# Two neighbouring keys per partition in a two-layer cross-attention kernel on one Trainium2 core

## The chip, the cores and the metric

The kernel runs on one core of one Trainium2 chip. The metric is the device time of one execution in microseconds (us); lower is better. The engines are named as the profile names them: PE is TensorE's matmul, PEld its weight load, DVE is VectorE, ACT ScalarE, POOL GpSimd, and SP is SyncE, whose queue issues nearly all loads from HBM. A stretch of the trace is given as the two times, in us from the start of the span, between which it lies.

## The reference

Two cross-attention layers are applied one after the other to `x` (8 batches, 100 tokens, 1024 features). Both attend to the same context `ctx_512` (8 batches, 1444 keys, 512 features). Everything is float32.

```
# layer 0
Q = x @ Wq + bq ; K = ctx @ Wk + bk ; V = ctx @ Wv + bv
w = softmax(Q @ K.T / 32, over the 1444 keys)
x = x + (w @ V) @ Wo + bo
# layer 1, with its own weights
q, k, v = as above
w = softmax(q @ k.T / 32, over the 100 tokens)
x = layer_norm(x + w @ v) * gamma + beta
```

The context appears in two roles. In the scores the sum runs over features, and each key is an output. In the weighted sum of the context the sum runs over keys. A sum over keys does not depend on the order in which the keys are taken, as long as the weights and the context rows use the same order.

## The kernel before, in words

**Algebra.** Keys and values are never formed. The product `Wq Wk^T` is made once per layer and applied to `x`, which gives for each token a query of 512 features, `gT[layer]`. Scores are then products of these queries with the raw context, and the weighted sums of the raw context (512 features per token, the tile `A`) are multiplied by `Wv` (layer 1) or `Wv Wo` (layer 0) behind the attention. The dense products use sub-products with fewer multiplications than the plain form.

**Order.** The span falls into these stages: weight products, queries and preparations of both layers (0 to 181 us), attention of layer 0 (181 to 306), output of layer 0 and queries of layer 1 (306 to 383), attention of layer 1 with its output in between (383 to 547), the last tokens (547 to 571). TensorE's instructions are in the order of the program (`manual_schedule` for PE). Loads of the context go through `loaded_in_order` (L947 to L955), which keeps them in program order on the SP queue and makes each wait, so that no more than `UNDER_WAY` (1800 KB), itself included, is on its way at any time:

```
while sum(size for _, size in under_way) > UNDER_WAY:
    latest, _ = under_way.pop(0)
```

**Two copies of the context.** For the scores the features must be on the partitions. The host gives the context also transposed, and `load_features` (L957) brings it as four tiles `cT` per batch, one per 128 features, each with all 1444 keys in its columns (two loads per tile in layer 0, four in layer 1). For the weighted sums the keys must be on the partitions. `load_rows` (L977) brings the context as it is, as four tiles `c` ("units") per batch. A unit holds three key tiles of 128 keys, side by side in the columns, 512 features each. So `c` has on partition p, key tile i of unit q, the key `384 q + 128 i + p`. The last unit holds two full key tiles and the last 36 keys. There are twelve key tiles m, numbered through: unit `m // 3`, place `m % 3`.

**Scores** (`scores_by_keys`, L1076 to L1109). For each of the four feature chunks k and each key tile m, the weights of the matmul are 64 columns of `cT[k]`, and the 100 queries of the batch are what moves through the array. A full key tile is made in two halves of 64 keys, one on each half of the array's columns, so that the two matmuls overlap in time. Scores of key tile m go to column block m of three PSUM banks, with the key's place in the tile as partition. A float32 matmul shows as two records in the trace, each with its own weight load. Softmax follows on DVE and ACT, and leaves the weights `w[p, m, token]`.

**Weighted sums** (`weighted_rows`, L1009 to L1059). For each key tile and feature chunk, 64 columns of `c` are the weights of the matmul and `w[:, m, :]` moves. Again there are two halves.

**Together** (`alternated`, L1533). Weighted sums of batch b and scores of batch b + 2 take turns on TensorE, a step of each at a time: 48 steps per batch, of four records of `A` (L1020) and four of `s` (L1092). The loads of batch b's rows and of batch b + 2's features take turns on the SP queue in the same way: the rows of one unit, then one feature tile (`loaded`, L1525).

Of the kernel before, what the change touches and what calls it, by code (L numbers as in the profile page):

```python
# [31 lines left out]
P = 128  # L32
HP = P // 2
# [5 lines left out]
CQ = MC // NQ  # L39
# [19 lines left out]
def two_layer_cross_attention(ctx: ExitStack, tc: tile.TileContext, a: dict, out: bass.AP):  # L59
# [11 lines left out]
    def bank(name):  # L71
        return psum.tile([P, 512], F32, tag="ps", name=name)
# [4 lines left out]
    def unit(name):  # L77
        return stream.tile([P, E + L], F32, tag="unit", name=name)

    def wide(name):  # L80
        return work.tile([P, LC, GT], F32, tag="AT", name=name, bufs=2)
# [4 lines left out]
    def weight_rows(name):  # L86
        return work.tile([P, MC * T], F32, tag="wT", name=name, bufs=3)
# [859 lines left out]
    def loaded_in_order(to, src):  # L947

        load = tc.keep_in_program_order(nc.sync.dma_start(out=to, in_=src)).ins
        under_way.append((load, 4 * math.prod(to.shape)))  # L950
        latest = None
        while sum(size for _, size in under_way) > UNDER_WAY:
            latest, _ = under_way.pop(0)
        if latest is not None:
            tc.add_manual_dep(load, latest.name, landed, reason="room among the transfers under way")  # L955

    def load_features(b, blocks=(2, 3), parts=2, order=range(LC)):  # L957

        bounds = [LAST * i // parts for i in range(parts)] + [S]

        for k in order:
            name = f"cT_{b}_{k}"
            t = feature_block(name) if k in blocks else unit(name)[:, :S]
            for part in (slice(i, j) for i, j in zip(bounds, bounds[1:])):
                loaded_in_order(t[:, part], a["ctxT"][b][k * P : (k + 1) * P, part])
            yield t

    def quarters_of(b):

        return (NQ - 1, *range(NQ - 1)) if b in SECOND else range(NQ)  # L970

    def last_rows(b):

        p0 = HP if b in SECOND else 0
        return slice(p0, p0 + S - LAST)

    def load_rows(b):  # L977

        src = a["ctx_512"][b]
        for q in quarters_of(b):  # L980
            t = unit(f"c_{b}_{q}").rearrange("p (c l) -> p c l", c=CQ)
            n = CQ - (q == NQ - 1)
            r0 = q * CQ * P
            for i in range(n):
                loaded_in_order(t[:, i, :], src[r0 + i * P : r0 + (i + 1) * P, :])
            if n < CQ:
                more = PAD - (S - LAST)
                loaded_in_order(t[last_rows(b), n, :], src[LAST:S, :])
                if b not in FIRST + SECOND:
                    loaded_in_order(t[S - LAST : PAD, n, :], src[:more, :])  # L990
            yield t

    def keys(m):

        return P if m < MC - 1 else S - LAST
# [3 lines left out]
    def both_sides():  # L999

        return side, 1 - side

    def one_side():

        nonlocal side
        side = 1 - side
        return (1 - side,)
# [68 lines left out]
    def scores_by_keys(s, layer, cT, softmax, hold=False):  # L1076

        b = s["b"]
        q = gT[layer][b // G]
        t0 = b % G * T  # L1080
        banks = [bank(f"s{layer}_{b}_{n}") for n in range(MC // GM)]
        rest = []
        for k in range(LC):
            for m in KEYS:
                whole = keys(m) == P
                n = HP if whole else keys(m)
                for h in both_sides() if whole else one_side():
                    o = m * P + h * HP if whole else m * P
                    to = banks[m // GM][h * HP : h * HP + n, m % GM * T : (m % GM + 1) * T]
                    if k >= LC - 2 and not whole:  # L1090
                        rest.append(to)
                    nc.tensor.matmul(  # L1092
                        to,
                        cT[k][:, o : o + n],
                        q[:, k, t0 : t0 + T],
                        start=(k == 0 and m % GM == 0),
                        stop=(k == LC - 1 or (k == LC - 2 and not whole)),
                        skip_group_check=True,
                    )
                if hold or (k, m) != (LC - 1, KEYS[-1]):  # L1100
                    yield
        w = weight_rows(f"w{layer}_{b}")
        s["w"] = w[:, : MC * T].rearrange("p (c t) -> p c t", t=T)
        if b not in FIRST + SECOND:
            nc.gpsimd.memset(s["w"][:PAD, MC - 1, :], 0.0)
        s["softmax"] = softmax(s, [blocks_of(banks, ms) for ms in ROWS], rest)
        for _ in islice(s["softmax"], LATER.get((layer, b))):
            pass
        yield  # L1109

    def blocks_of(banks, ms):

        m, n, r = ms[0], len(ms), keys(ms[0])
        ps = banks[m // GM][:r, m % GM * T : (m % GM + n) * T]
        return ms, slice(0, r), ps.rearrange("p (c t) -> p c t", t=T)
# [417 lines left out]
    def alternated(b, layer, softmax, dst, first=0, got=None):  # L1533

        nxt = b + 2 < B
        rows = batches[b].pop("rows", None) or load_rows(b)
        c, *cT = got or loaded(rows, *([load_features(b + 2, parts=4 if layer else 2)] if nxt else []))
        if b in FIRST:
            other, more = batches[b + 1], load_rows(b + 1)
            other["first"] = next(more)  # L1540
            other["rows"] = chain([other["first"]], more)
        A = weighted_rows(batches[b], layer, c, dst)
        ahead = scores_by_keys(batches[b + 2], layer, *cT, softmax) if nxt else iter(())
        run(islice(ahead, first))
        for n in range(MC * LC):
            if n < (LC * (MC - 1) if b in FIRST else LC * MC):
                next(A, None)
            next(ahead, None)
            if n == LC * MC - 1:
                next(A, None)  # L1550
            yield

    cT = [list(load_features(0))]
    block, *more = load_features(1, (2,), order=(2, 0, 1, 3))
    cT.append([*more[:2], block, *more[2:]])
    c0, more = list(load_rows(0)), load_features(2)
    cT.append([next(more)])
    scores0 = scores_by_keys(batches[0], 0, cT[0], softmax0)
    run(islice(scores0, 3 * MC + 6))
    run(key_bias_rows(kb0, part0, bqbk0))  # L1560
    run(scores0)
    cT[2] += more
    block_sums("u1", acc_u, sums[:, :LC, :], late=True)
    block_sums("wqbk1", acc_c, sums[:, LC : LC + EC, :], late=True)
    run(scores_by_keys(batches[1], 0, cT[1], softmax0))
    for b in range(B):
        dst = A0[b // G][:, :, b % G * T : (b % G + 1) * T]
# [44 lines left out]
    cT = [list(load_features(0, parts=4)), list(load_features(1, (2,), 4))]  # L1612
    result = out.rearrange("b t e -> (b t) e")
    n = TILES[-1][0] // 6
# [32 lines left out]
    for b in range(B):  # L1647
        parts = []
        for last, _, tokens in SETS:
# [3 lines left out]
            if last not in homes:  # L1653
                t = wide(f"A1T_{last}").rearrange("p c t -> p (c t)")[:, : LC * len(tokens)]
# [52 lines left out]
```

## Time and profile before

| | us |
|---|---|
| median of 3 runs | 571.9 |
| lowest and highest | 570.89 and 572.43 |
| the profiled execution's own time | 573.0 |
| its span, first to last instruction | 571.2 |

Stages of the profiled execution, as busy times in us:

| stretch | PE | PEld | DVE | DMA share | GB/s |
|---|---|---|---|---|---|
| 0 to 181 | 179.85 | 143.29 | 152.49 | 0.86 | 234 |
| 306 to 383 | 77.00 | 53.50 | 60.63 | 0.60 | 198 |
| 547 to 571.2 | 16.51 | 13.13 | 14.51 | 0.28 | 56 |

The two stages of attention are shown with the prediction. Loads of the context in the profile, by size and with the median time from issue to landing:

| load | count | KB each | us to landing |
|---|---|---|---|
| rows, one key tile of 128 keys | 176 | 256 | 4.8 |
| rows, the last 36 keys | 16 | 72 | |
| features, layer 0, columns 0 to 703 | 32 | 352 | 4.7 |
| features, layer 0, columns 704 to 1443 | 32 | 370 | 4.6 |
| features, layer 1, three parts of 352 columns | 96 | 176 | 4.7 |
| features, layer 1, the last 388 columns | 32 | 194 | 4.8 |

How to read it: the mean of a group in the profile is the time of one instruction from its start to its end, not what it adds to the stream. Matmuls and weight loads overlap in time, so a group's mean is longer than its step; the step is read from the starts in the timeline. The busy time is the union of such intervals. A waiting time is put down to the instruction or landing that ended it; "issue" means that the profile shows nothing that it waited for. The DMA share is the mean busy share of the core's 16 DMA engines.

### The profile page before, as it was taken

How to read it: one execution, taken by the hardware profiler on the slowest of the kernel's cores; microseconds unless marked ns; L12 is line 12 of the kernel's file. 1: busy time of each engine (PE TensorE's matmuls, PEld its weight loads, DVE VectorE, ACT ScalarE, POOL GpSimd, SP SyncE). 2: the span in 40 equal slices, each digit the busy share in tenths (PEclk: the TensorE clock that was granted, in tenths of full speed). 3: DMA queues.
4: the chain of work that ended last, by engine and by line, in shares of the span. 5: the costliest groups of instructions: out<-in, count | busy, mean ns of one | idle time of the engine just before them, and what ended most of it. 6: DMA issues, size and time to landing. Idle time of an engine off the chain costs nothing.

```text
span 571.2 us, 17345 instructions
## 1 busy us (share of the span) xinstructions
PE 560.2 (98%) x7328; PEld 471.2 (82%) x7328; DVE 453.2 (79%) x1051; ACT 146.0 (26%) x383; POOL 112.9 (20%) x171
## 2 busy tenths in 40 slices
PE   9999999999999999999999999999999999999994
PEld 8887567668999989999997856679999869959672
DVE  2997979878999794886457687799788779879865
ACT  1331321356020112202111000121433035336632
POOL 3110110222100043142222000000421312403232
PEclk9999999999999999999999999999999999999998
DMA  9959989958938999899999503985899969985804
GB/s 287 318 109 322 309 208 279 318 90 199 254 66 296 331 330 332 293 325 328 326 329 318 196 1 129 288 298 189 253 293 336 341 208 325 312 271 169 220 5 92
DMA packets 73390, 141.24 MB, mean 247 GB/s; under 512 B 8160, under 2 KB 29920, under 8 KB 73312
## 3 DMA queue, kind: packets, MB, share of 16 engines
q1 hardware_dynamic: 66592, 121.40, 62.6%
q0 software_dynamic: 6288, 18.20, 16.5%
q8 instruction: 58, 0.95, 0.7%
q10 hardware_dynamic: 432, 0.52, 0.3%
q14 instruction: 20, 0.16, 0.1%
HBM read 123.49 MB, written 6.03 MB: 227 GB/s over the span
## 4 chain that ended last, share of the span: by engine, by line
PE 77%; DMA 18%; issue 2%; DVE 1%; SPq 1%; POOL 1%; ACT 1%; DVEq 0%; POOLq 0%
DMA cT<-in_ctxT 14%; PE A L1020 14%; PE s L1092 12%; PE qk_x L170 7%; PE g_x L170 6%; PE vo_x L170 4%; DMA c<-in_ctx 4%; PE o_x L170 3%; PE o_x L1343 3%; PE qk_z L170 2%; PE g_y L170 2%; PE o_y L1343 2%; PE o_y L170 1%; PE qk_w L170 1%; PE qk_y L170 1%
## 5 line engine op out<-in xcount | busy, mean ns | idle before, releaser
L1020 PE MATMUL A<-w,c 128*64 128x100 f32 (+2 forms) x3072 | 217.0, 249 | 1.7 <-issue 1.7
L1020 PEld LDWEIGHTS A<-w,c 128*64 128x64 f32 (+2 forms) x3072 | 190.1, 137 | 4.8 <-issue 3.6
L1092 PE MATMUL s<-g1T,cT 128*64 128x100 f32 (+1 forms) x1472 | 109.5, 249 | 0.0
L1092 PE MATMUL s<-g0T,cT 128*64 128x100 f32 (+1 forms) x1472 | 108.3, 249 | 0.5 <-DMA cT<-in_ctxT 0.5
L1092 PEld LDWEIGHTS s<-g1T,cT 128*64 128x64 f32 (+1 forms) x1472 | 94.9, 136 | 0.8 <-DMA cT<-in_ctxT 0.6
L1092 PEld LDWEIGHTS s<-g0T,cT 128*64 128x64 f32 (+1 forms) x1472 | 94.2, 136 | 1.0 <-DMA cT<-in_ctxT 0.7
L1310 POOL TENSOR_TENSOR part<-w 128x500 f32<-128x500 f32 x16 | 25.3, 1584 | 237.0 <-DVE rtotal L102 77.9
L1288 ACT ACTIVATE w<-w,negmax 128x100 f32<-128x100 f32 x96 | 34.9, 365 | 44.5 <-DVE negmax L102 44.2
L1156 ACT ACTIVATE w<-w 128x400 f32<-128x400 f32 (+2 forms) x32 | 12.8, 447 | 115.5 <-DVE w L102 104.7
L102 DVE STREAM_TRANSPOSE z<-xT 32x256 f32<-32x256 f32 x88 | 38.3, 435 | 1.4
L170 PE MATMUL qk_x<-qk 128*128 128x256 f32 x160 | 37.8, 380 | 0.0
L170 PEld LDWEIGHTS qk_x<-qk 128*128 128x128 f32 x160 | 28.9, 190 | 3.4 <-ACT qk L444 0.2
L1073 DVE RECIPROCAL rrow<-A 128x100 f32<-128x100 f32 x8 | 6.2, 770 | 22.7 <-PE A L1064 22.6
L170 PE MATMUL vo_x<-vo 128*128 128x512 f32 x48 | 23.3, 594 | 0.0
L102 DVE TENSOR_REDUCE most<-s 128x100 f32<-128x400 f32 (+1 forms) x24 | 12.6, 525 | 10.9 <-PE s L1092 10.3
L102 DVE TENSOR_TENSOR w<-w,rtotal 128x400 f32<-128x400 f32 (+2 forms) x32 | 18.2, 567 | 1.1
L102 DVE SCALAR_TENSOR_TENSOR w<-s,kb 128x400 f32<-128x400 f32 (+2 forms) x32 | 14.3, 464 | 5.4 <-PE s L1092 5.1
L742 ACT ACTIVATE g1T<-g_x,k 128x400 f32<-128x400 f32 x4 | 2.4, 593 | 61.0 <-PE g_x L170 60.9
L1288 ACT ACTIVATION_READ_ACCUMULATOR w<-w,negmax 128x1 f32 x96 | 17.9, 187 | 0.0
L1313 POOL TENSOR_TENSOR part<-part 128x100 f32<-128x100 f32 x32 | 15.8, 493 | 2.5
L102 DVE TENSOR_TENSOR qk<-qk 128x256 f32<-128x256 f32 (+2 forms) x27 | 14.9, 579 | 0.0
L170 PE MATMUL qk_z<-qk 128*128 128x256 f32 x64 | 14.1, 379 | 0.0
(490 smaller groups left out, 1010.2 us busy)
## 6 DMA issues: line engine op xcount, KB each, us to landing
c<-in_ctx SPq DMA_DIRECT2D x176, 256.0 KB, 4.8
cT<-in_ctxT SPq DMA_DIRECT2D x96, 176.0 KB, 4.7
cT<-in_ctxT SPq DMA_DIRECT2D x32, 370.0 KB, 4.6
cT<-in_ctxT SPq DMA_DIRECT2D x32, 352.0 KB, 4.7
cT<-in_ctxT SPq DMA_DIRECT2D x32, 194.0 KB, 4.8
vo<-in_L_xattn_Wo SPq DMA_DIRECT2D x8, 512.0 KB, 9.0
qk<-in_L_xattn_WqT SPq DMA_DIRECT2D x8, 512.0 KB, 6.3
qk<-in_L_xattn_WqT SPq DMA_DIRECT2D x15, 256.0 KB, 4.9
```

The costliest lines, as they stand in the source:

```text
L102: ins = getattr(nc.vector, op)(*args, **kw)
L170: nc.tensor.matmul(banks[n // per][:, n % per * width : (n % per + 1) * width], lhs[i][:, n * P : (n + 1) * P], rhs[i], start=(fresh and i ...
L742: nc.scalar.activation(dst[g][:, c, :], banks[j][:, :GT], AF.Identity, bias=u[:, c : c + 1])
L1020: nc.tensor.matmul(ps[h * HP : (h + 1) * HP, k * T : (k + 1) * T], block[rows, m % CQ, k * P + h * HP : k * P + (h + 1) * HP], s["w"][rows ...
L1073: nc.vector.reciprocal(r, ps[:, GT : GT + T])
L1092: nc.tensor.matmul(to, cT[k][:, o : o + n], q[:, k, t0 : t0 + T], start=(k == 0 and m % GM == 0), stop=(k == LC - 1 or (k == LC - 2 and no ...
L1156: nc.scalar.activation(rows, rows, AF.Exp)
L1288: ins = nc.scalar.activation(rows[:, i, :], rows[:, i, :], AF.Exp, bias=negmax[:, i : i + 1], accum_out=total[:, i : i + 1])
L1310: add(part, w[:, 0:5, :], w[:, 5:10, :], ALU.add)
L1313: add(part[:, 0, :], part[:, 0, :], more, ALU.add)
L1343: nc.tensor.matmul(ps[:n, :], lhs[0][:, i, :], rhs[0][:, i, :], start=(fresh and i == 0), stop=(i == 1), skip_group_check=True,)
```

## The change

In `load_rows` the first two key tiles of each unit are loaded with one transfer of 256 keys, viewed so that partition p takes the two neighbouring keys `384 q + 2 p` and `384 q + 2 p + 1`. The first goes to place 0, the second to place 1; the two keys are 4096 contiguous bytes in HBM and in the partition. The third key tile, where there is one, and the last 36 keys are loaded as before. The number of bytes is the same.

In `scores_by_keys` the order of the scores follows. For places 0 and 1 of a unit (m = 0, 1, 3, 4, 6, 7, 9 and 10) the weights are taken from a block of 256 columns of `cT[k]`, every second column, beginning at column 0 or 1 of the block; the 128 columns of a key tile are again cut in two halves of 64. For place 2 (m = 2, 5, 8) and for the last 36 keys the columns are contiguous as before. Number, shape and order of all matmuls are the same, and so are softmax and weighted sums in the program's text.

```
@@ load_rows
-            for i in range(n):
-                loaded_in_order(t[:, i, :], src[r0 + i * P : r0 + (i + 1) * P, :])
+            pair = src[r0 : r0 + 2 * P, :].rearrange("(p c) l -> p c l", c=2)
+            loaded_in_order(t[:, :2, :], pair)
+            if n > 2:
+                loaded_in_order(t[:, 2, :], src[r0 + 2 * P : r0 + n * P, :])
@@ scores_by_keys
-                    o = m * P + h * HP if whole else m * P
+                    block = cT[k][:, m * P : m * P + keys(m)]
+                    if whole:
+                        if m % CQ < 2:
+                            o = m // CQ * CQ * P
+                            block = cT[k][:, o : o + 2 * P].rearrange("p (i c) -> p c i", c=2)[:, m % CQ, :]
+                        block = block[:, h * HP : (h + 1) * HP]
...
                     nc.tensor.matmul(
                         to,
-                        cT[k][:, o : o + n],
+                        block,
                         q[:, k, t0 : t0 + T],
```

## The prediction

> **What bounds the kernel now.** I read the page first, then the busy time by stage, then the waits of TensorE and of the SP queue, then TensorE's timeline at its longest data wait, and last the matmul and weight-load groups by shape.
>
> ```profile
> PE 560.2 (98%) x7328; PEld 471.2 (82%) x7328; DVE 453.2 (79%) x1051; ACT 146.0 (26%) x383; POOL 112.9 (20%) x171
> PE 77%; DMA 18%; issue 2%; DVE 1%; SPq 1%; POOL 1%; ACT 1%; DVEq 0%; POOLq 0%
> ```
>
> TensorE is busy for 98% of the span, so 11.0 us at most are idle in it. Yet 18% of the chain that ended last is DMA: two resources are nearly balanced. The stages say where (columns: us, then busy us and count of each engine, granted clock, DMA share, GB/s):
>
> ```profile
> 181.00:306.00 125.00, 122.80 (x2855) 121.09 (x2853) 89.01 (x234) 19.58 (x40) 31.56 (x52) 1.00 0.96 323
> 383.00:547.00 164.00, 164.00 (x2949) 140.16 (x2948) 136.59 (x308) 59.99 (x237) 42.03 (x66) 1.00 0.80 256
> ```
>
> The first row is the attention of layer 0, the second that of layer 1; the granted clock is full in both. In layer 0 the DMA engines are busy for 96% and TensorE lacks 2.2 us; in layer 1 TensorE lacks nothing. All that TensorE waits for behind the start is this:
>
> ```profile
> PE A L1020 <- issue: 1.7, 2, 1.2
> PE s L1092 <- DMA cT<-in_ctxT: 0.5, 1, 0.5
> SPq L949 <- DMA cT<-in_ctxT: 40.9, 43, 3.1
> SPq L949 <- DMA c<-in_ctx: 18.0, 33, 2.4
> ```
>
> The two last lines are the SP queue in 181 to 306: it waits 58.9 us for room among the transfers under way, not for buffers. The one data wait stands at the end of 107 us of full DMA:
>
> ```profile
> 287.77 0.34 PE L1020 MATMUL A<-w,c 128*64 128x100 f32 x4
> 287.95 0.34 PE L1092 MATMUL s<-g0T,cT 128*64 128x100 f32 x4
> 288.12 0.34 PE L1020 MATMUL A<-w,c 128*64 128x100 f32 x4
> 288.99 0.39 PE L1092 MATMUL s<-g0T,cT 128*64 128x100 f32 x4 [0.53 <-DMA cT<-in_ctxT]
> ```
>
> Groups of four records start every 0.171 us: 42.8 ns a record, 85.6 ns for a pair, one on each column half (matmuls of 64 columns on the two halves overlap). The group at 288.99 was due at 288.29: 0.7 us lost. One batch of layer 0 loads 2888 KB of rows and 2888 KB of features, 5.91 MB, 18.3 us at 323 GB/s; TensorE needs 48 steps of 0.342 us, 16.4 us. So the lead won before 181 us melts by about 1.9 us a batch and is gone at 288 us. That matters twice: a faster DMA can win back 0.7 us and no more, a slower one is paid nearly in full.
>
> **The change: the weight loads.** Each matmul here has two records and two weight loads (92 matmuls a batch, 1472 records in 8 batches). In 8 of 11 full key tiles the weights come from every second column: 8 x 2 sides x 4 chunks x 2 records x 16 = 2048 records, 1024 pairs. Count, shape and order stay. What a load costs:
>
> ```profile
> L1092 PEld LDWEIGHTS s<-g0T,cT 128*64 128x64 f32 x1408 | 90.4, 137 | 1.0 <-DMA cT<-in_ctxT 0.7
> L1092 PEld LDWEIGHTS s<-g0T,cT 128*36 128x36 f32 x64 | 6.4, 113 | 0.0
> L170 PEld LDWEIGHTS qk_q_x<-qk 128*128 128x128 f32 x48 | 6.0, 192 | 0.1
> ```
>
> The mean goes 113, 137, 192 ns for 36, 64, 128 columns: 0.86 ns per column on both steps, so 64 columns take 55 ns and the rest is latency. It has to fit under one record of the same half, 85.6 ns. A strided load may therefore take 85.6/55 = 1.56 times as long and cost nothing; what hides it is the matmul running on that half, and behind 1.56 each extra ns is paid by every pair. No load of before is strided, so I bound it. Below: nothing; a gain is excluded, as the column count is the same and loads already end in time. Above: twice the time, 110 ns; the nearest row is a load of 128 columns under 128 moving ones, whose eight records start 0.89 us apart, 111 ns each. 111 - 85.6 = 25.4 ns, x 1024 = 26 us. The Trainium skill, "SBUF — State Buffer", section on the DMA port swizzle, has the rule that speaks against the change: SBUF is read in lines of 16 bytes, an access that crosses to a new line pays, and full rate needs two or more accesses per line. Unit stride gives four float32 per line, every second column two: crossings double, the condition is just met. By its limit the term is 0, by its penalty up to 26 us. No run here shows which. I take 0, since rule and 1.56 would both have to fail, and keep 26 us as the far end.
>
> **The transfers.** Per batch and layer the row loads go from 11 of 256 KB (and the small ends) to 4 of 512 KB and 3 of 256 KB; bytes are the same. The SP queue saves 64 issues in all at a median of 402 ns (the rows' tile view), 26 us of its time; worth nothing, since it waits for landings anyway. Each row packet becomes 4096 bytes instead of two of 2048. In the trace's packet records of 182 to 289 us a 2048-byte packet takes 94.1 ns on average, 84 ns in the median; 4096-byte packets of the same queue, elsewhere in this trace, 159 ns in the median. Ratio 159/168: two rows go from 188 to 178 ns. 8238 row packets fall in that stretch, 8/11 paired: about 3000 pairs x 10 ns / 16 engines = 1.9 us. The Trainium skill, "DMA: Bandwidth & Descriptors", "Why small descriptors are slow", gives about 3 cycles a packet beside one per 32 bytes: 131 instead of 134, 2.2%, estimate 0.8 us. Measurement first, 1.9; but the sum is the same by either, for both cover the 0.7 us wait and there is nothing further to win. Where that wait goes, TensorE itself is next.
>
> **The added granularity.** The first tile of a unit now waits for 512 KB: it can start 256 KB / 323 GB/s = 0.8 us later, if rows are what comes last. They aren't: no wait for c is in TensorE's list, and each unit's rows are issued ahead of the feature tile needed at the same step, which decides. With room for 1800 KB, a steady cycle of 352, 370, 256, 256, 256 KB leaves at least 1120 KB in flight while SP waits; with the pair it is 978 KB when the next pair is to go. Behind a waiting pair stand its third tile and the next feature loads. 978 KB is 3.1 us of work, against 2.5 us from issue to landing of the fastest load: still covered, cost 0; with the cover gone see below.
>
> Other edits are nil: buffers, softmax and the final row ends keep their order; a sum over keys doesn't mind their permutation. The two "issue" stops (2.1 us between starts, at 202 and 301, each inside a group of four, so no data) I leave.
>
> **Sum.** Weight loads 0, data wait -0.7, granularity 0. Profiled: span 571.2 to 570.5, run 573.0 to 572.3. That run lies 1.1 above the median of 571.9, so I predict 571.2 us.
>
> **The rivals.** *Strided weight loads are slower than the matmul that covers them.* For: PEld is busy for 121 of 125 us in layer 0, the cover is 31 ns wide, and line crossings double. Against: two accesses per line and room for 1.56 times. From 1.56 on it decides; at twice, 26 us: 597 us; at 1.75 times, 96 ns, 11 us: 582.
>
> *The coarser queue starves the DMA engines.* For: SP spends 76 waits on landings in 125 us, the cycle is DMA-bound, and 978 KB leave just 0.6 us of margin. A bubble of 0.2 us in each of some 20 cycles is 4 us, all paid: about 575. Against: 64 fewer issues, longer packets.
>
> *More than the wait is won.* If emptier queues also end the two "issue" stops, 2.1 us more go: 569.1. For: both lie where DMA is full. Against: nothing ties them to context data.
>
> *The change does nothing to the packets* (the pair is still cut into rows): 571.9, no change.
>
> **How the numbers follow.** 0.3%, 1.7 us, is about what a measurement of this kernel can tell from no change. Covered loads with the won wait: 0.40, of which 0.35 same and 0.05 faster by spread. Packets unchanged: 0.05, same. More won, some part of the stops: 0.21, all faster. Starved DMA: 0.12, 0.10 slower and 0.02 same. Slow weight loads: 0.22, all slower, a third of it below 580. Sums: faster 0.26, same 0.42, slower 0.32. The range starts at 569.2, leaving out 0.04, and ends at 580, leaving out about 0.15 of slow loads; the covered cases alone are 569.2 to 573.
>
> **What would show it.** Right: strided loads may read longer than 137 ns, but groups in layer 0 still start 0.171 us apart; row packets of 4096 bytes, about 8200 fewer packets; the wait at 288 us is gone; DMA share a little under 0.96. Wrong by the first rival: groups of scores start more than 0.171 us apart in key tiles 0, 1, 3, 4, 6, 7, 9, 10 and not in 2, 5, 8, and both attention stages grow alike. By the second: pace kept, but new waits of TensorE for c or cT in layer 0 alone, with the DMA share below 0.95.

## The result, and the profile after

The changed kernel takes 576.02 us (median of 11 runs, 572.53 to 578.85), the kernel before 571.89 us in the same session (median of 11). The ratio is 1.0061, with a 95% interval from 1.0037 to 1.0085: slower by 3.5 us, between 2.1 and 4.9 (the two medians lie 4.1 us apart). Forecast were 571.2 us and no change; the range (569.2 to 580) holds the result, the direction is not the one forecast. The profiled execution took 575.32 us with a span of 573.5 us, close to the median. Two of the six runs by halves of the partitions were more than 1.5% slower than the fastest of them and are left out of its numbers.

The page of the changed kernel, busy times and the chain that ended last:

```profile
PE 561.1 (98%) x7328; PEld 471.8 (82%) x7328; DVE 452.7 (79%) x1051; ACT 145.9 (25%) x383; POOL 113.1 (20%) x171
PE 88%; DMA 7%; issue 1%; DVE 1%; POOL 1%; ACT 1%; SPq 0%; DVEq 0%; POOLq 0%
```

TensorE's busy time is 0.9 us higher and the span 2.3 us longer, so most of the loss is idle time. The share of DMA in the chain fell from 18% to 7%, although DMA is what got worse. In both traces the chain leaves TensorE at its last wait for data and follows the loads back from there; before, it stays with them from 289 to 182 us, after, only from 292 to 250 us, where a load had waited 0.3 us for a buffer that TensorE freed, and it returns to TensorE. This share does not measure what DMA costs. The busy time by stage does better (us, then busy us and count of PE, PEld, DVE, ACT, POOL, granted clock, DMA share, GB/s):

```profile
181.00:306.00 125.00, 121.07 (x2799) 119.14 (x2799) 85.79 (x223) 18.09 (x36) 31.10 (x51) 1.00 0.91 310
383.00:547.00 164.00, 164.00 (x2950) 140.94 (x2950) 138.47 (x310) 59.84 (x236) 39.91 (x61) 1.00 0.82 263
```

In the attention of layer 0 the DMA engines are busy for 91% of the time instead of 96% and move 310 GB/s instead of 323. Over 125 us that is 1.6 MB less, 5 us of transfers. TensorE lacks 3.9 us there, all for data, instead of 2.2, of which 0.5 were for data. In layer 1 it lacks nothing, before or after. TensorE's waits for data, of its list of waits (us in total, times, longest):

```profile
PE s L1099 <- DMA cT<-in_ctxT: 3.9, 5, 1.2
```

And what the SP queue waits for in 181 to 306, in the same columns:

```profile
SPq L949 <- DMA c<-in_ctx: 48.4, 29, 3.3
SPq L949 <- DMA cT<-in_ctxT: 23.6, 30, 1.8
```

There was one data wait of 0.5 us; now there are five, 3.9 us. SP's waits for landed rows went from 18.0 us to 48.4 us, with fewer of them: a wait for a pair is long. In sum SP waits for 72.0 us instead of 58.9, while the DMA engines move less. The last of the five waits in TensorE's timeline:

```profile
290.55 0.25 PE L1022 MATMUL A<-w,c 128*64 128x100 f32 x1
290.63 0.25 PE L1099 MATMUL s<-g0T,cT 128*64 128x100 f32 x1
290.64 0.41 PE L1022 MATMUL A<-w,c 128*64 128x100 f32 x3
292.29 0.39 PE L1099 MATMUL s<-g0T,cT 128*64 128x100 f32 x4 [1.24 <-DMA cT<-in_ctxT]
292.51 0.34 PE L1022 MATMUL A<-w,c 128*64 128x100 f32 x4
```

It stands at a score, not at a weighted sum: the rows, whose loads were changed, arrive in time, and the feature tile queued behind them comes late.

The trace's packet records show where the DMA engines ran dry. In the mean over 18 pairs between 195 and 282 us their busy share falls to 0.78, 0.71 and 0.66 in the second, third and fourth quarter of a microsecond after SP issues the pair; in the kernel before it is 0.91 or more in the first 1.25 us after the first row load of a unit. In the records one can also count what is issued and not yet moved. When SP issues a pair, that is 463 KB in the mean (19 pairs between 195 and 286 us), though the program counts 978 KB as under way: the rest had been moved, and SP had not yet acted on its landing. In the kernel before the least is 676 KB in the mean, where the program counts 1120 KB (ahead of the 370 KB feature loads).

The weight loads of the scores, every second column in 8 of 11 key tiles, by shape (busy us, mean ns, idle before):

```profile
L1099 PEld LDWEIGHTS s<-g0T,cT 128*64 128x64 f32 x1408 | 92.8, 138 | 5.1 <-DMA cT<-in_ctxT 4.1 <-DVE rrow L1075 0.8
L1099 PEld LDWEIGHTS s<-g1T,cT 128*64 128x64 f32 x1408 | 91.0, 138 | 0.8 <-issue 0.8
```

Their matmuls in layer 1, by shape, before and after:

```profile
L1092 PE MATMUL s<-g1T,cT 128*64 128x100 f32 x1408 | 105.2, 249 | 0.0
L1099 PE MATMUL s<-g1T,cT 128*64 128x100 f32 x1408 | 105.2, 249 | 0.0
```

The groups show 138 ns in the mean instead of 137, with single loads of up to 144 ns instead of 138, and the matmuls of layer 1 are busy for 105.2 us as before.

### The profile page after: what moved, and what is told of

It reads as the page before. It is cut to its first block, busy times and chain, and to the rows that moved or that the text cites. A ratio compares the mean times of both kernels' runs of the same rounds, so it can differ in the third digit from the quotient of the medians.

```text
span 573.5 us, 17272 instructions
## 1 busy us (share of the span) xinstructions
PE 561.1 (98%) x7328; PEld 471.8 (82%) x7328; DVE 452.7 (79%) x1051; ACT 145.9 (25%) x383; POOL 113.1 (20%) x171
## 4 chain that ended last, share of the span: by engine, by line
PE 88%; DMA 7%; issue 1%; DVE 1%; POOL 1%; ACT 1%; SPq 0%; DVEq 0%; POOLq 0%
PE s L1099 19%; PE A L1022 18%; PE qk_x L170 7%; DMA cT<-in_ctxT 6%; PE g_x L170 6%; PE vo_x L170 4%; PE o_x L170 3%; PE o_x L1350 3%; PE qk_z L170 2%; PE g_y L170 2%; PE o_y L1350 2%; PE o_y L170 1%; PE qk_w L170 1%; PE qk_y L170 1%; PE vo_z L170 1%
## 5 line engine op out<-in xcount | busy, mean ns | idle before, releaser
L1022 PEld LDWEIGHTS A<-w,c 128*64 128x64 f32 (+2 forms) x3072 | 192.6, 137 | 2.7 <-issue 1.5
L1099 PEld LDWEIGHTS s<-g0T,cT 128*64 128x64 f32 (+1 forms) x1472 | 96.7, 137 | 5.1 <-DMA cT<-in_ctxT 4.1
```

The costliest lines, as they stand in the source:

```text
L1022: nc.tensor.matmul(ps[h * HP : (h + 1) * HP, k * T : (k + 1) * T], block[rows, m % CQ, k * P + h * HP : k * P + (h + 1) * HP], s["w"][rows ...
L1099: nc.tensor.matmul(to, block, q[:, k, t0 : t0 + T], start=(k == 0 and m % GM == 0), stop=(k == LC - 1 or (k == LC - 2 and not whole)), ski ...
```

## The experiments

The theories: (1) the 512 KB transfer makes the room of 1800 KB too coarse, so that too little is in flight when SP may issue again; (2) 4096-byte packets are served more slowly; (3) strided weight loads cost time. Two more came up on the way: (4) reading every second row of HBM, (5) TensorE's own instructions delayed by a deep queue. Each ratio is against runs of the kernel before beside it, with medians of 571.6 to 571.7 us.

**More room for the changed kernel.**

```
-UNDER_WAY = 1800 * 1024
+UNDER_WAY = 2056 * 1024
```

> The changed kernel with room for 2056 KB instead of 1800 KB among the transfers under way, nothing else. In a steady cycle of the layer-0 attention this leaves at least 1490 KB in flight while SP waits, where the changed kernel leaves 978 KB and the kernel before 1120 KB. Theory 1 (the 512 KB transfer makes the room too coarse, the DMA engines run dry): the data waits of TensorE in 181 to 306 us (3.9 us) go to under 1 us, DMA share there back from 0.91 to 0.96 or more, time 570.5 to 572. Theory 2 (packets of 4096 bytes are served more slowly under load): waits and time stay as in the changed kernel, 575 to 576. Theory 3 (strided weight loads cost time): also 575 to 576, with no wait behind it.

Measured: 571.99 us, ratio 1.0007 (0.9979 to 1.0034). The stage of layer 0:

```profile
181.00:306.00 125.00, 125.00 (x2867) 122.86 (x2866) 90.84 (x238) 19.57 (x40) 32.58 (x52) 1.00 0.97 341
```

All that TensorE waited for in this execution:

```profile
PE warm L114 <- DVE ones L111: 1.1, 1, 1.1
PE ol L1510 <- ACT A1T L1037: 0.4, 1, 0.4
```

No wait for data is left, and the same packets and the same weight loads run at 341 GB/s. A pair now finds 906 KB left to move in the mean, and the dip behind its issue is gone. Theory 1 holds. Theories 2 and 3 fall as causes of the loss.

**The big transfer alone, in the kernel before.** One transfer of 512 KB for two key tiles, each key at its old place: packets of 2048 bytes, contiguous weight loads.

```
-            for i in range(n):
-                loaded_in_order(t[:, i, :], src[r0 + i * P : r0 + (i + 1) * P, :])
+            loaded_in_order(t[:, :2, :], src[r0 : r0 + 2 * P, :].rearrange("(c p) l -> p c l", c=2))
+            if n > 2:
+                loaded_in_order(t[:, 2, :], src[r0 + 2 * P : r0 + n * P, :])
```

> The kernel before with its first two key tiles of each unit in one transfer of 512 KB, each key where it was: 2048-byte packets, contiguous weight loads. Theory 1: as slow as the changed kernel or slower, 575 to 577, with data waits at cT in layer 0 of 4 us or more. Theory 2: as the kernel before, 572. Theory 3: as the kernel before, 572.

Measured: 577.24 us, ratio 1.0102 (1.0061 to 1.0142). Its stage of layer 0:

```profile
181.00:306.00 125.00, 121.48 (x2799) 119.55 (x2800) 86.58 (x224) 18.09 (x36) 31.02 (x51) 1.00 0.92 306
```

TensorE's waits for data:

```profile
PE s L1093 <- DMA cT<-in_ctxT: 3.4, 3, 1.7
```

SP's waits in 181 to 306:

```profile
SPq L949 <- DMA c<-in_ctx: 46.1, 28, 3.1
SPq L949 <- DMA cT<-in_ctxT: 26.0, 34, 1.6
```

This is the picture of the changed kernel without its packets or its strides: the size of the transfer does it. A pair finds 515 KB left to move. The kernel comes out 0.4% slower than the changed one, but the two intervals overlap. In 200 to 285 us its 2048-byte packets take 99.9 ns in the mean, two of them 199.8 ns, and a 4096-byte packet of the changed kernel 197.7 ns: in the same coarse queue the longer packets are not the slower ones, which speaks against theory 2 a second time.

**Strided weight loads alone.** The changed scores with the row loads of before.

```
-            pair = src[r0 : r0 + 2 * P, :].rearrange("(p c) l -> p c l", c=2)
-            loaded_in_order(t[:, :2, :], pair)
-            if n > 2:
-                loaded_in_order(t[:, 2, :], src[r0 + 2 * P : r0 + n * P, :])
+            for i in range(n):
+                loaded_in_order(t[:, i, :], src[r0 + i * P : r0 + (i + 1) * P, :])
```

> The changed scores with the loads of the kernel before: every second column in the weight loads of two key tiles in three, rows in 256 KB transfers of contiguous keys. The weighted sums therefore pair weights with other keys' rows than the reference does. Theory 1 (only the loads matter): as the kernel before, ratio 1.000, groups of four records 0.171 us apart everywhere. Theory 3 (strided weight loads cost, in pace or by slowing the DMA writes into the same memory): 574.5 to 576, that is all of what the run with two transfers of 256 KB lost.

Measured: 571.73 us, ratio 1.0005 (0.9988 to 1.0021). The weight loads of this kernel:

```profile
L1097 PEld LDWEIGHTS s<-g1T,cT 128*64 128x64 f32 x1408 | 91.0, 138 | 0.8 <-DMA cT<-in_ctxT 0.6 <-issue 0.2
```

They read 138 ns as in the changed kernel, and cost nothing that these runs can tell (0.2% at most): theory 3 is out. The one profiled execution was the longest of the 14 (574.73 us, with 2.0 us of data waits), which shows how far a single trace may lie from the median here; the ratio rests on the timed runs.

**The least or the mean in flight.** The kernel before with less room, and the changed kernel with a little more.

```
-UNDER_WAY = 1800 * 1024
+UNDER_WAY = 1656 * 1024        # kernel before
+UNDER_WAY = 1944 * 1024        # changed kernel
```

> The kernel before with room for 1656 KB instead of 1800 KB. In the steady cycle 1234 KB instead of 1490 KB are in flight where SP waits ahead of the row loads, and 1120 KB at the least as before. Theory 1, if the mean in flight counts: slower by 2 to 5 us, with waits at cT in layer 0. Theory 1, if only the least counts: no change, 572. Theories 2 and 3: no change, 572.

> The changed kernel with room for 1944 KB: 1490 KB in flight at three of the four loads of the cycle, but still 978 KB when the next pair is to go. Theory 1 with the least in flight: as the changed kernel, 575 to 576. Theory 1 with the mean in flight: most of the loss is gone, 572 to 573.5.

Measured: 573.36 us, ratio 1.0032 (1.0014 to 1.0050), for the kernel before at 1656 KB; 574.20 us, 1.0042 (1.0025 to 1.0059), for the changed kernel at 1944 KB. At 1656 KB only the row loads see less in flight (1234 KB instead of 1490 KB), the least is the same 1120 KB, and still 0.3% is lost (1.8 us, a little under the 2 to 5 expected): the least is not all that counts. At 1944 KB three of four loads see 1490 KB and only the pair still 978 KB. The time lies between the two forecasts, 572 to 573.5 and 575 to 576, and about a third of the loss is gone by the ratios; but the interval overlaps that at 1800 KB, so that this share is not shown. What the trace shows is that the pair still finds little left to move there, 549 KB.

**Two transfers of 256 KB in the new order.** Even keys, then odd keys, with 2048-byte packets; once with the changed scores and once with the scores of before.

```
-            loaded_in_order(t[:, :2, :], pair)
+            for i in range(2):
+                loaded_in_order(t[:, i, :], pair[:, i, :])
```

> The changed kernel with the pair of keys loaded by two transfers of 256 KB, one for the even and one for the odd keys: same places, same strided weight loads, but 2048-byte packets and the transfer sizes of the kernel before. Theory 1: as the kernel before, 571.5 to 572.5. Theory 2: the same, 571.5 to 572.5. Theory 3: as the changed kernel, 575 to 576.

> The kernel before with only the row loads changed: the first two key tiles of each unit take even and odd keys, in two transfers of 256 KB with 2048-byte packets from every second row; scores as before, so the weighted sums pair weights with other keys' rows than the reference does. Theory 4 (reading every second row of HBM is what made the run with two transfers of 256 KB slow): 574 to 576, with waits at cT in layer 0 of 4 us. Theory 3: as the kernel before, 572.

Measured: 574.83 us, ratio 1.0047 (1.0021 to 1.0073), and 574.39 us, ratio 1.0044 (1.0021 to 1.0066). The first was a miss for theories 1 and 2, which gave 572, and looked like theory 3. The second has contiguous weight loads and loses the same, so it is the reading of every second 2048-byte row that costs 0.4%, at unchanged sizes (theory 4). TensorE's data waits in the profiled execution with the changed scores:

```profile
PE s L1100 <- DMA cT<-in_ctxT: 4.6, 4, 1.6
```

and in that with the scores of before, which ran below its median (572.27 us):

```profile
PE s L1094 <- DMA cT<-in_ctxT: 1.5, 2, 0.7
```

They stand at the feature tiles again. The first of these traces was the longest run of its kernel (577.60 us), and its stage of layer 0 looks like that of the changed kernel:

```profile
181.00:306.00 125.00, 120.27 (x2774) 118.45 (x2775) 85.56 (x221) 18.08 (x36) 31.03 (x51) 1.00 0.92 309
```

So a DMA share of 0.92 alone does not tell a coarse queue from another reason; the runs that change one thing do. Why every second row is slower than neighbouring rows was not tried. The changed kernel doesn't read so: its pairs are contiguous.

**Two transfers of 256 KB by halves of the partitions.** 4096-byte packets, 64 partitions each.

```
-            loaded_in_order(t[:, :2, :], pair)
+            for h in range(2):
+                loaded_in_order(t[h * HP : (h + 1) * HP, :2, :], pair[h * HP : (h + 1) * HP])
```

> The changed kernel with the pair of key tiles loaded by two transfers of 256 KB, one per half of the partitions: packets of 4096 bytes of neighbouring keys as in the changed kernel, but the transfer sizes of the kernel before and so its room (at least 1120 KB in flight). Theory 1 (size of the transfer, not of the packet): 571 to 572.5, ratio within 0.2% of 1. If a half of the partitions is served by fewer ways into the memory, slower than the changed kernel: 577 or more.

Measured: 612.98 us, ratio 1.0738 (1.0690 to 1.0786). The stage of layer 0:

```profile
181.00:306.00 125.00, 106.95 (x2322) 103.69 (x2322) 74.77 (x191) 16.34 (x32) 27.35 (x44) 0.97 1.02 255
```

TensorE's waits for data:

```profile
PE s L1100 <- DMA cT<-in_ctxT: 25.7, 16, 3.7
```

The row loads in the list of DMA issues (KB each, median us to landing):

```profile
c<-in_ctx SPq DMA_DIRECT2D x176, 256.0 KB, 6.7
```

The 571 to 572.5 us of theory 1 were missed by far. The 176 loads are 128 of a half and 48 of all partitions. In 200 to 285 us a 4096-byte packet takes 274 ns in the mean instead of 198 in the changed kernel, and the 2048-byte packets of the whole loads 149 instead of 97: everything in the queue is slower. The DMA engines are full all the time and move only 255 GB/s. This is another loss than that of the changed kernel, whose engines run dry; the run says nothing on theory 1, and it closes this way to get long packets in small transfers.

**More room for the kernel before, and much room for both.**

```
-UNDER_WAY = 1800 * 1024
+UNDER_WAY = 1944 * 1024        # kernel before; also 2056 and 2312
+UNDER_WAY = 2312 * 1024        # changed kernel
```

> The kernel before with room for 2056 KB. At least 1490 KB are then in flight instead of 1120 KB. Theory 1: the DMA share in layer 0 rises to 0.97, the wait of 0.5 us at cT goes, time lower by 0 to 1.5 us. If it comes out as the changed kernel with the same room, the 4096-byte packets bring nothing once the room is wide.

> The kernel before with room for 1944 KB: 1490 KB in flight at each load of the cycle. Theory 1: as with 2056 KB, 570.5 to 571.5; if later code is what a wide room costs, a little better than with 2056 KB.

> The changed kernel with room for 2312 KB. Theory 1: TensorE has no wait on data in layer 0 as with 2056 KB, so nothing more is won: 570.5 to 572. If transfers under way that are too many hurt (longer from issue to landing, so later landing of what is needed first, or instruction code that comes later), it is slower than with 2056 KB: 573 or more.

> The kernel before with room for 2312 KB. Theory 5 (a deep queue delays TensorE's own instructions, which are loaded by the same DMA engines): no data waits in layer 0, but issue waits of several us that end 1 to 2 us after a 16 KB instruction packet has landed, time 573 to 577, as with the changed kernel. If the 4096-byte packets were what delays instructions: no such waits, 570.5 to 571.5.

| room, KB | kernel before | changed kernel |
|---|---|---|
| 1656 | 1.0032 (1.0014 to 1.0050) | |
| 1800 | 1 | 1.0061 (1.0037 to 1.0085) |
| 1944 | 0.9983 (0.9972 to 0.9995) | 1.0042 (1.0025 to 1.0059) |
| 2056 | 0.9983 (0.9972 to 0.9995) | 1.0007 (0.9979 to 1.0034) |
| 2312 | 1.0035 (1.0019 to 1.0051) | 1.0093 (1.0061 to 1.0124) |

Both kernels are best at a middle width. The kernel before gains 0.17% at 1944 or 2056 KB; these are the only versions faster than both kernels, and the changed kernel doesn't pass them at any width tried. At 2056 KB it lies 0.24% above the kernel before, but the intervals overlap, so what its packets and strides are worth in a full queue stays open. Too wide costs time as well, but with another wait. The changed kernel at 2312 KB, stage of layer 0:

```profile
181.00:306.00 125.00, 119.50 (x2715) 117.49 (x2716) 83.10 (x215) 18.08 (x36) 31.02 (x51) 0.99 0.94 336
```

Its TensorE's waits, without the start and the end:

```profile
PE A L1022 <- issue: 5.2, 5, 2.2
PE s L1099 <- issue: 1.0, 2, 0.5
```

The same of the kernel before at 2312 KB:

```profile
PE s L1092 <- issue: 1.2, 1, 1.2
```

No wait for data is left at 336 GB/s, yet 6.2 us of "issue" stand in the changed kernel: stops with no releaser. This trace was the longest of six runs (580.65 us). In its packet records, five of the stops in layer 0 (0.7 to 2.4 us between starts) each end 1.3 to 1.5 us after a 16 KB packet of the instruction queue has landed; that packet had started 6.2 to 7.6 us after the one before it, while they are 5.8 us apart on average from 189 us on. The one stop of the kernel before at 2312 KB ends 1.4 us behind such a packet too, and so do the two stops at 202 and 301 us in the first profile (1.4 and 1.6 us). The constant distance suggests that TensorE had run out of code, which came late behind more data in the same DMA engines. It is not shown: no run took the code loads away, intervals of 7.2 to 7.5 us stand without a stop in both kernels at 2056 KB, and one stop of 1.2 us in a run of 572.73 us does not account for the median of 573.80 us of the kernel before at 2312 KB.

## Why the prediction was wrong

- *The added granularity* is the step that failed. It took 978 KB in flight for 3.1 us of work, set them against 2.5 us, the fastest landing in the whole trace, and put the cost at 0; it measured 3.5 us. Both sides were wrong. Of the 978 KB that the program counts, 463 KB were left to move when the pair was issued, 1.5 us at 323 GB/s. And the landing of 2.5 us belongs to the attention of layer 1, where the DMA share is 0.80; in the attention of layer 0 the fastest took 3.8 us. The engines were not quite full before the change either: share 0.96 with 676 KB left to move at the least issue, 0.99 with 902 KB (the kernel before at 2056 KB).
- *The bound it rests on* was right in its second half: a slower DMA is paid nearly in full. DMA fell behind by 5 us of transfers, TensorE waited 3.9 us for data, all of it from 271 us on, when the lead was used up. The first half, that a faster DMA can win back 0.7 us and no more, is compatible with the 0.17% (0.05 to 0.28%, that is 0.3 to 1.6 us) that the kernel before wins at 1944 and 2056 KB.
- *The transfers*: 1.9 us were expected from 4096-byte packets that take 5% less than two of 2048 bytes. One took 197.7 ns instead of 199.8 for two at 1800 KB (against the kernel before with the pair in one transfer), and 179 instead of 185 at 2056 KB. So 1 to 3% were there; in time nothing of it was seen at any width.
- *The weight loads* were right: cost 0, shown alone by 1.0005 (0.9988 to 1.0021). The rule of the Trainium skill, "SBUF — State Buffer", section on the DMA port swizzle (two accesses per line keep the full rate), agrees with the 138 ns; since 1.56 times would have been hidden as well, the 138 ns and not the unchanged total confirm it.
- *The rivals*: "the coarser queue starves the DMA engines" named place, price (4 us, about 575) and signs (waits for cT in layer 0 alone, DMA share below 0.95) and is what happened. Even its bubble of 0.2 us a cycle fits: between 195 and 285 us the share is 0.912 instead of 0.956, 4 us in 19 pairs. TensorE paid for it late, in five stops of 0.9 to 1.5 us between starts. It had a chance of 0.12, because its margin of 0.6 us came from the two wrong figures above. Of the prediction's own signs the pace came true (groups start at 200.24, 200.41 and 200.59 us, 0.171 us apart), and so did the 4096-byte packets.
- *The "issue" stops*, left without a cause, were absent from the changed kernel's trace, as the third rival had hoped, and nothing was won. They end at the same distance behind a code packet as those with wide room; but the kernel before has two at 1800 KB, none at 1944 and 2056 KB and one at 2312 KB, in one trace each, so the width alone does not decide, and their cause stays open.

## What to carry to other kernels

A limit in bytes on transfers under way belongs together with the size of a transfer: when transfers get larger, what is left in flight at the moment of the next issue gets smaller, so widen the limit with them and measure both sides of its best width. The program's own count of what is under way is too high, here by half when the pair was issued; count in the packet records what is issued and not yet moved. Landing times are a poor mark: the fastest may come from a quieter stage, and the median of the same loads grows with the room (256 KB of rows in layer 0 of the kernel before: 5.1 us at 1800 KB, 5.3 at 2056, 5.8 at 2312). Where DMA and TensorE are nearly balanced, read the DMA share and GB/s of that stage; the share of DMA in the chain can fall while DMA gets worse.

## What the runs showed of the hardware

- When SP issued a load of 512 KB with 978 KB counted as under way, 463 KB of them were left to move in the mean, and the DMA engines' busy share fell to 0.66 within 1 us behind the issue.
- A queue in which most row loads of 256 KB go into 64 partitions instead of 128 moved 255 GB/s at full DMA busy time, where other full queues of these runs moved 323 to 344; the packets of its 128-partition loads were slower too (149 ns instead of 97).
- Reading every second 2048-byte row costs 0.4% of the kernel against reading neighbouring rows, with the same packets and transfer sizes.
- Weight loads of 64 float32 columns, with a step of two columns in 8 of 11 key tiles, take 138 ns in the mean instead of 137.
- Eight stops of TensorE of 0.7 to 2.4 us, in three traces, ended 1.3 to 1.6 us after a 16 KB packet of the instruction queue had landed.
